# Layer norm of the first token tile: statistics partly on ScalarE, one set of factors, another order of the halves

## The chip, the core and the metric

The kernel runs on one core of a Trainium2 chip. The metric is the device time of one execution in microseconds. A core has five engines that run side by side, each through its own queue in order: PE (TensorE, matrix products and transposes; PEld is its loading of weights), DVE (VectorE), ACT (ScalarE), POOL (GpSimd) and SP, which here only issues transfers. They wait for one another by semaphores. SBUF is the memory that all engines work in, PSUM holds what PE writes, in banks of 128 x 512 values.

## What is computed

2 x 1024 tokens of 512 features, all in float32. Each token is normalised over its features (layer norm). Two paths use the result: a linear layer with a block-masked weight, and a gated feed-forward network with an RMS norm ahead of it. Their product is added to the input.

```python
def _layernorm(x, axis=-1, eps=1e-05):
    m = jnp.mean(x, axis=axis, keepdims=True)
    v = jnp.var(x, axis=axis, keepdims=True)
    return (x - m) / jnp.sqrt(v + eps)

# attn: out = einsum('bsk,nk->bsn', data, weight * block_mask)
# ffn:  nx = x * rsqrt(mean(x*x) + 1e-5) * ln_w
#       g, u = nx @ gate_w.T, nx @ up_w.T          (1792 wide)
#       out = (silu(g) * u) @ down_w.T
xn = _layernorm(L0_attn_data)
s = attn(xn)
g = silu(ffn(xn))
return L0_attn_data + s * g
```

## The kernel before

The 2048 tokens are four token tiles t of 512, each four row tiles i of 128 tokens. A row tile lies in SBUF with tokens on the partitions and 512 features along them. The products need features on the partitions, so a normalised row tile is transposed by PE in four chunks c of 128 features; a chunk of a whole token tile fills one PSUM bank (`pt`, 128 x 512) and is copied to SBUF (`evacuate`).

The products follow Strassen's scheme in Winograd's form, at two levels: instead of eight block products it takes seven and sums of blocks. One outer product q of one group g of weights is an *instance* j; an instance is seven inner products m of 128 x 128 by 128 x 512, which accumulate in banks x, y and z (`instance`, line 395 the product). Instance 0 works on chunks 0 and 1, instance 1 on chunks 2 and 3. In this text x0 is the first product of instance 0, in bank x, with chunk 0 of token tile 0; z0 is its product with chunk 1; x1 and z1 are those of instance 1 with chunks 2 and 3. The later products (y0 and so on) need token tile 1 as well, and differences of chunks that DVE and POOL make (`inner_b`). Bank y of instance 1 (y1) is the one that z1 leaves. The gate weights of both instances are scaled by the RMS weight ahead of use (`scale_a`, line 314 on POOL), and sums of their quarters are made on POOL (`inner_a`, line 98).

Only token tiles 0 and 1 take the way of this text, in the head of the kernel; tiles 2 and 3 follow later under running products. For a tile of the head the steps are:

- `load_x` (line 127): four transfers of 256 KB by SP's queue.
- `stats(t, i)` (lines 131, 132): DVE's bn_stats and bn_aggr give mean and variance of a row tile, into `agg`.
- `factors(t, i, n)` (lines 150, 147, 148): ACT takes the root of the variances of n row tiles, DVE the reciprocal `scl` and the shift `nb`. Token tile 0 has two sets, of row tiles 0, 1 and 2, 3; token tile 1 has one.
- `normalise(t, i, eng, cols)` (line 158 on ACT, line 156 on DVE): half a row tile, 256 features, in place.
- `transpose(t, c, i, tag)` (line 165) and `evacuate(t, c, eng)` (line 173).

Nothing is scheduled by a tool: `at(pos, fn)` notes an event with a position, and at the end the events are issued in order of position. Every engine's queue is the order of its instructions in that list. `T(us)` turns a time into a position, and the list `EARLY` moves single products and copies of the first two instances ((j, m) a product, (j, 0) the seed copy of x). So a position sets the order on an engine, not a time.

Before the head's first real work PE runs products of a unit matrix (`warm`, line 756). On POOL a 1-element memset (line 742) holds back SP's later loads.

Of the kernel before, what the change touches and what calls it, by code (L numbers as in the profile page):

```python
# [8 lines left out]
F32 = mybir.dt.float32  # L9
I32 = mybir.dt.int32  # L10
AF = mybir.ActivationFunctionType
ALU = mybir.AluOpType
AX = mybir.AxisListType

P = 128
W = 512
# [15 lines left out]
def tile_masked_linear_gated_ffn(  # L32
# [11 lines left out]
    nc = tc.nc  # L44
# [15 lines left out]
    small = ctx.enter_context(tc.tile_pool(name="small", bufs=2))  # L60
# [6 lines left out]
    EARLY = {}  # L67

    def at(pos, fn, *args):
        events.append((pos, len(events), fn, args))  # L70
# [5 lines left out]
    mem = big.tile([P, sum(n for _, n in RINGS), W], F32, tag="mem", name="mem")  # L76
# [5 lines left out]
    F = first_slot  # L82
# [6 lines left out]
    def slots(i, n):  # L89
        return mem[:, i : i + n, :]  # L90
# [3 lines left out]
    def bank(tag, name):  # L94
        return ps.tile([P, W], F32, tag=tag, name=name, bufs=PSB[tag])

    def add(eng, o, a, b, op=ALU.add):
        eng.tensor_tensor(o, a, b, op)  # L98

    dve, pool, act = nc.vector, nc.gpsimd, nc.scalar  # L100
# [18 lines left out]
    xt, raw, stat = {}, {}, {}  # L119
    agg = small.tile([P, NTT, TT, 2], F32, tag="agg", name="agg", bufs=1)  # L120
# [8 lines left out]
    def stats(t, i):  # L129
        st = small.tile([P, 6], F32, tag="st", name=f"st_{t}_{i}")  # L130
        nc.vector.bn_stats(st, xt[t, i])  # L131
        nc.vector.bn_aggr(agg[:, t, i, :], st)

    def factors(t, i=0, n=TT):


        if t < 2:
            scl = small.tile([P, n], F32, tag="scl", name=f"scl_{t}_{i}", bufs=3)
            nb = small.tile([P, n], F32, tag="nb", name=f"nb_{t}_{i}", bufs=3)
        else:  # L140
            scl, nb = fac[:, t - 2, 0, :], fac[:, t - 2, 1, :]
        for k in range(n):
            stat[t, i + k] = (scl[:, k : k + 1], nb[:, k : k + 1])
        rows = slice(i, i + n)

        def last():
            nc.vector.reciprocal(scl, scl)
            nc.vector.scalar_tensor_tensor(nb, agg[:, t, rows, 0], -1.0, scl, ALU.mult, ALU.mult)

        return [lambda: nc.scalar.activation(scl, agg[:, t, rows, 1], AF.Sqrt, bias=eps2, scale=1.0 + EPS), last]  # L150

    def normalise(t, i, eng, cols=slice(0, W)):
        scl, nb = stat[t, i]
        v = xt[t, i][:, cols]
        if eng is dve:
            nc.vector.tensor_scalar(v, v, scl, nb, ALU.mult, ALU.add)
            return
        nc.scalar.activation(v, v, AF.Identity, bias=nb, scale=scl)  # L158

# [137 lines left out]
    def w_slots(g):  # L297

        return (F["s"], F["s"] + 5) if g % 2 else (F["q"], F["a1"] + 4)
# [28 lines left out]
    def outer_a(g):  # L328


        b = wblk[g]
        v = {}

        def in_bank(k, K):
            v[k] = bank("V", f"a{k}_{g}")
            scaled(v[k], b[k], g, K)

        return [lambda: scaled(b[2], b[1], g, 0), lambda: scaled(b[4], b[4], g, 1), lambda: in_bank(1, 0),
                lambda: in_bank(0, 0), lambda: add(dve, b[1], v[1], b[4]),
                lambda: add(dve, b[2], v[0], b[2], ALU.subtract), lambda: add(dve, b[0], b[1], v[0], ALU.subtract),  # L340
                lambda: in_bank(3, 1), lambda: add(dve, b[3], v[3], b[0], ALU.subtract)]
# [17 lines left out]
    def mask_a(v, R, K):  # L359
        v = v.rearrange("p (b j) -> p b j", j=BLK)  # L360
        k = keep[:, 2 * R + K, :].unsqueeze(2).to_broadcast([P, 16, BLK])
        nc.gpsimd.tensor_tensor(v, v, k, ALU.mult)

    def inner_a(g, part, k0=0, n=2):

        if part == 1:
            i, si, qs = F["a1"] + 2 * (g % 3), F["s"] + 2 * (g % 2), (1, 2)
        else:
            i, si, qs = *w_slots(g), BLOCKS
        a, s = slots(i + k0, n), slots(si + k0, n)  # L370
        a11, a21, a12, a22 = (a[:, :, k * P : (k + 1) * P] for k in range(4))
        s1, s2, s3, s4 = (s[:, :, k * P : (k + 1) * P] for k in range(4))
        for k in range(n):
            aop[g, qs[k0 + k]] = {1: a11[:, k], 2: a12[:, k], 3: s4[:, k], 4: a22[:, k],
                                  5: s1[:, k], 6: s2[:, k], 7: s3[:, k]}
        return [lambda: add(pool, s1, a21, a22), lambda: add(pool, s2, s1, a11, ALU.subtract),
                lambda: add(pool, s4, a12, s2, ALU.subtract), lambda: add(pool, s3, a11, a21, ALU.subtract)]
# [258 lines left out]
    def down_instance(o, q, where_, prior, dest, after):  # L636
# [78 lines left out]
        if last_set:  # L715
            at(where_(17) + 0.1, base_of_last)
            for part, pos in zip(parts, (where_(23), where_(24), where_(25))):
# [9 lines left out]
    N = len(order)  # L727
    END = 7 * N
    T = lambda us: (us - 14.0) / 0.86
    EARLY.update({(0, 1): T(10.4), (0, 2): T(11.3), (1, 1): T(12.1), (1, 2): T(13.0), (0, 0): T(11.5), (1, 0): 4.3,  # L730
                  (0, "z"): 2.2, (1, "z"): 4.5})
    SILU = 26.2
    at(T(-10), constants)
# [5 lines left out]
    at(T(-10), load_x, 1)  # L739
    at(T(-10), load_a, 0, 1)  # L740

    at(T(9.95), lambda: nc.gpsimd.memset(mem[:, F["a1"] + 2, 0:1], 0.0))
    for K in range(2):
        at(T(9.96), load_a, 1, K)
    at(T(9.96), load_x, 2)
    for K in range(2):
        at(T(9.96), load_a, 2, K)
    at(T(9.96), load_x, 3)
    def plan(pos, step, todo):
        for i, fn in enumerate(todo):  # L750
            at(pos + step * i, fn)


    def warm(n, b):
        for _ in range(n):
            nc.tensor.matmul(b[:, :P], ident, ident, start=True, stop=True, skip_group_check=True)

    at(T(1.4), lambda: warm(22, bank("V", "idle")))
    plan(T(4.9), 0, factors(0, 0, 2))
    plan(T(7.1), 0, factors(0, 2, 2))  # L760
    for t, p, step in ((1, T(12.5), 0), (3, 23.2, 0.6), (2, 36.1, 1.2)):
        plan(p, step, factors(t))
    for us, i, h in ((5.9, 0, 0), (6.0, 0, 1), (6.1, 1, 0), (7.2, 1, 1), (7.95, 2, 0), (8.4, 2, 1), (7.95, 3, 0), (8.4, 3, 1)):
        at(T(us), normalise, 0, i, dve if i == 3 else act, slice(h * W // 2, (h + 1) * W // 2))
    for i in range(TT):
        half = act if i < 2 else dve
        at(T(3.7 + 0.82 * i), stats, 0, i)
        at(T(9.35 + 0.82 * i), stats, 1, i)
        for h, cols in enumerate((slice(0, W // 2), slice(W // 2, W))):
            at(T(13.45 + 0.9 * h + 0.4 * (i % 2)), normalise, 1, i, half, cols)  # L770
        for c in range(KC):
            at(T((8.9, 9.3, 9.8, 11.0)[c] + 0.05 * i), transpose, 0, c, (0, 1, 3, 2)[i], "XYYX"[c])
            at((T(14.35), T(14.8), T(15.25), 4.1)[c] + 0.06 * i, transpose, 1, c, (2, 3, 0, 1)[i], "XVVV"[c])
    at(T(6.0), scale_a, 0, 0, pool)
    at(T(10.0), scale_a, 0, 1, pool)
    for c in range(KC):
        at(T((9.75, 10.3, 10.85, 12.05)[c]), evacuate, 0, c, act)
        at((5.6, 2.09, 6.0, 5.05)[c], evacuate, 1, c, act)
    for pos, q, m, eng in ((1.1, 1, 5, dve), (1.87, 1, 6, dve), (2.56, 1, 7, dve), (3.95, 2, 5, dve), (2.7, 1, 4, pool),
                           (5.06, 2, 6, dve), (10.05, 2, 7, dve), (5.07, 2, 4, pool)):  # L780
# [16 lines left out]
    for n, p0 in ((1, 31), (0, 50)):  # L797
        t = 2 + n
# [24 lines left out]
    for g in range(G + 1):  # L823
        p, rest = 7 * where[g, 1], 7 * where[g, BLOCKS[0]]
        for K in range(2):
            if g > 2:
                at(p - 22, load_a, g, K)
            if g == G:
                at(p - (10.4, 7.3)[K], lambda K=K: mask_a(aq[G, 0, K], 0, K))
            elif g > 1:  # L830
                at(p - (10.4, 7.3)[K], scale_a, g, K)
        if g:
            plan(p - 7, 1, inner_a(g, 1))
        else:
            plan(T(9.9), 0, inner_a(0, 1, 0, 1))
            plan(2.75, 0, inner_a(0, 1, 1, 1))
        at(rest - 29, load_block, g)

        def block_sums(g=g):
            for k, fn in enumerate(outer_a(g)):  # L840
                todo[g, k] = fn
        at(rest - 20, block_sums)
        if g == G:
            for k, (R, K) in ((1, (1, 0)), (4, (1, 1)), (0, (0, 0)), (3, (0, 1))):
                at(rest - 20.5, lambda k=k, R=R, K=K: mask_a(wblk[G][k], R, K))
        for k, off in enumerate((-19.9, -19.3, -18.1, -17, -15.95, -15.94, -15.93, -15.3, -13.95)):
            at(rest + off, lambda g=g, k=k: todo[g, k]())
        plan(rest - 13, 2.5, inner_a(g, 2, 0, 5))
# [138 lines left out]
```

## Time and profile before

| what | us |
|---|---|
| time, median of 3 runs (lowest, highest) | 506.41 (506.39, 506.83) |
| span of the profiled execution, first to last instruction | 504.8 |
| PE busy in 0 to 8.2 us | 6.83 |
| PE busy in 497.4 to 504.8 us | 3.49 |
| row tiles of token tile 0: last landing event of each | 3.48, 4.16, 4.95, 5.58 |
| first weights (instance 0), second (instance 1): landed | 7.29, 11.07 |
| mean of a bn_stats, a bn_aggr (DVE) | 0.67, 0.18 |
| mean of a half row tile normalised on ACT, on DVE | 0.59, 0.42 |
| mean of a chunk's copy on ACT | 0.59 |
| mean of half a weight tile scaled on POOL | 0.96 |
| mean of one 128 x 128 sum on POOL | 0.46 |

The profiled execution is one of its own; the times come from other executions, and their median lies 1.6 us over its span. Lines of a profile are read as: line of the kernel, engine, operation, tile written <- tiles read, shape. PE pieces x2 are the two passes of one float32 product. What an engine waited for is given in brackets with the idle time before it. Instructions of ACT and DVE overlap their neighbours a little, so that a start may lie ahead of the end before it.

### The profile page before, as it was taken

What the parts mean: (1) busy time and instruction counts of PE and PEld (TensorE: products, weight loads), DVE (VectorE), ACT (ScalarE), POOL (GpSimd) and SP (SyncE); (2) the same over time, 40 slices, a digit from 0 to 9 for tenths busy, and PEclk for the clock granted to TensorE, in tenths of its full rate; (3) what the DMA queues carried; (4) which work ended last, traced back from release to release, by engine and by line L of the source; (5) the groups of instructions that cost most, each with busy time, mean ns of one, the idle gap of its engine ahead of it and who ended that gap; (6) DMA issues with size and microseconds to landing.
All of it is one profiled execution on the core that took longest, in us unless ns stands there. A gap on an engine that the chain in (4) does not pass through costs nothing.

```text
span 504.8 us, 4923 instructions
## 1 busy us (share of the span) xinstructions
PE 499.2 (99%) x1231; PEld 227.4 (45%) x1231; DVE 375.6 (74%) x578; ACT 188.1 (37%) x362; POOL 358.8 (71%) x301
## 2 busy tenths in 40 slices
PE   8999999999999999999999999999999999999996
PEld 7444444444444444444444444444444444444444
DVE  6887887876968969697896969879657644377636
ACT  6667775734535363443535333330101101001111
POOL 5629997464886959879696999985672764649960
PEclk9999999999999999999999999999999999999999
DMA  6878746368178594876949475599996798467362
GB/s 208 306 234 335 292 168 250 123 251 293 62 245 295 186 329 181 295 240 244 335 154 317 179 265 213 216 351 387 365 335 221 253 389 311 130 238 269 106 229 84
DMA packets 62221, 124.75 MB, mean 247 GB/s; under 512 B 5968, under 2 KB 13552, under 8 KB 60144
## 3 DMA queue, kind: packets, MB, share of 16 engines
q1 hardware_dynamic: 62048, 124.43, 69.1%
q8 instruction: 10, 0.16, 0.1%
q14 instruction: 19, 0.16, 0.1%
q10 hardware_dynamic: 144, 0.00, 0.0%
HBM read 78.25 MB, written 46.15 MB: 246 GB/s over the span
## 4 chain that ended last, share of the span: by engine, by line
PE 97%; DVE 1%; ACT 1%; DMA 1%; issue 0%; DVEq 0%; ACTq 0%
PE x L395 38%; PE y L395 19%; PE dx L643 15%; PE z L395 10%; PE dy L643 8%; PE dz L643 5%; PE dv L643 1%; PE pt L165 1%; DMA mem<-in_x 1%; DVE mem L98 0%; ACT mem L158 0%; DVE st L131 0%; DVE mem L633 0%; ACT silu L626 0%; ACT scl L150 0%
## 5 line engine op out<-in xcount | busy, mean ns | idle before, releaser
L98 POOL TENSOR_TENSOR mem<-mem 128x512 f32<-128x512 f32 (+4 forms) x261 | 322.1, 1257 | 111.6 <-ACT mem L423 30.5
L395 PE MATMUL x<-mem 128*128 128x512 f32 x448 | 211.7, 593 | 0.0
L395 PEld LDWEIGHTS x<-mem 128*128 128x128 f32 x448 | 84.6, 190 | 107.3 <-issue 89.7
L98 DVE TENSOR_TENSOR mem<-x,mem 128x512 f32<-128x512 f32 x137 | 93.4, 686 | 42.1 <-PE x L395 40.4
L395 PE MATMUL y<-mem 128*128 128x512 f32 x224 | 114.6, 593 | 0.1
L643 PE MATMUL dx<-mem 128*128 128x512 f32 x174 | 78.3, 592 | 0.0
L98 DVE TENSOR_TENSOR mem<-mem 128x1536 f32<-128x1536 f32 (+3 forms) x50 | 66.9, 1342 | 6.9 <-PE dx L643 4.4
L98 DVE TENSOR_TENSOR mem<-y,mem 128x512 f32<-128x512 f32 x96 | 65.9, 686 | 7.9 <-PE y L395 6.5
L402 ACT COPY z<-x 128x512 f32<-128x512 f32 x54 | 30.9, 573 | 94.7 <-PE x L395 91.7
L395 PEld LDWEIGHTS y<-mem 128*128 128x128 f32 x224 | 42.2, 190 | 53.1 <-issue 46.5
L395 PE MATMUL z<-mem 128*128 128x512 f32 x112 | 57.3, 593 | 0.0
L643 PEld LDWEIGHTS dx<-mem 128*128 128x128 f32 x174 | 33.1, 190 | 41.6 <-issue 40.9
L643 PE MATMUL dy<-mem 128*128 128x512 f32 x98 | 44.5, 592 | 0.0
L461 ACT ACTIVATE gate<-mem 128x512 f32<-128x512 f32 x56 | 32.7, 602 | 20.4 <-DVE mem L98 15.9
L466 DVE TENSOR_TENSOR mem<-gate,mem 128x512 f32<-128x512 f32 x56 | 38.1, 682 | 1.9 <-ACT gate L461 1.5
L616 POOL TENSOR_TENSOR mem<-mem 128x512 f32<-128x512 f32 x16 | 25.8, 1619 | 13.6 <-DMA mem<-s_dram 13.4
L626 ACT ACTIVATE silu<-mem 128x512 f32<-128x512 f32 x15 | 9.0, 602 | 64.6 <-DVE mem L98 48.3
L395 PEld LDWEIGHTS z<-mem 128*128 128x128 f32 x112 | 21.1, 190 | 25.9 <-issue 21.4
L98 DVE TENSOR_TENSOR mem<-z,mem 128x512 f32<-128x512 f32 x41 | 28.1, 685 | 2.8 <-PE z L395 2.7
L643 PEld LDWEIGHTS dy<-mem 128*128 128x128 f32 x98 | 18.6, 190 | 23.4 <-issue 23.2
L98 DVE TENSOR_TENSOR mem<-dx,mem 128x512 f32<-128x512 f32 x16 | 11.1, 691 | 20.3 <-PE dx L643 20.2
L643 PE MATMUL dz<-mem 128*128 128x512 f32 x56 | 25.2, 592 | 0.0
(86 smaller groups left out, 286.9 us busy)
## 6 DMA issues: line engine op xcount, KB each, us to landing
h_dram<-mem SPq DMA_DIRECT2D x98, 256.0 KB, 2.2
mem<-h_dram SPq DMA_DIRECT2D x28, 768.0 KB, 6.7
mem<-in_gu SPq DMA_DIRECT2D x42, 256.0 KB, 3.9
acc_dram<-mem SPq DMA_DIRECT2D x8, 1024.0 KB, 4.0
mem<-acc_dram SPq DMA_DIRECT2D x8, 1024.0 KB, 6.1
mem<-in_x_t SPq DMA_DIRECT2D x24, 256.0 KB, 5.5
mem<-in_x SPq DMA_DIRECT2D x16, 256.0 KB, 4.5
s_dram<-mem SPq DMA_DIRECT2D x16, 256.0 KB, 6.1
```

Source lines behind the costliest of these rows:

```text
L98: eng.tensor_tensor(o, a, b, op)
L165: nc.tensor.transpose(pt[t, c][:, i * P : (i + 1) * P], xt[t, i][:, c * P : (c + 1) * P], ident)
L395: nc.tensor.matmul(st[key], weights(g, q, m), operand(q, m), start=first and not (key == "z" and seeded), stop=True, skip_group_check=True)
L402: nc.scalar.copy(st["z"], st["x"])
L461: nc.scalar.activation(gate[key], t(), AF.Silu)
L466: nc.vector.tensor_mul(a(), gate[key], b())
L616: at_later.append(lambda: nc.gpsimd.tensor_tensor(s_tile, s_tile, rms_bc[t], ALU.mult))
L626: nc.scalar.activation(b[0][:, part], y[:, part] if source is None else source(), AF.Silu)
L643: nc.tensor.matmul(st[key], w(), b(), start=first and key != "z", stop=True, skip_group_check=True)
```

## The change

The statistics of row tile 1 of token tile 0 are made by ACT (`stats_act`): a pass with Identity whose accumulator gives minus the scaled mean, a pass with Square, shifted by it, whose accumulator gives the variance, and a one-column multiply for the mean. The passes write scratch values into a slot that is free then. DVE makes the other three. Token tile 0 has one set of factors for its four row tiles. The halves are normalised in another order, and one of them (row tile 1, second half) by POOL. The transposes have positions of their own: of chunks 2 and 3, row tile 0 comes ahead of x0, row tiles 1, 2 and 3 come behind z0. The seed copy of x0 moves behind the normalising of token tile 1. On POOL two of the four weight sums of instance 0 move behind the scaling of the second weights, and the memset and the loads that it holds back have new positions. `warm` has 21 products instead of 22. DVE's statistics of token tile 1 come earlier in the list.

```diff
+    shift = small.tile([P, 1], F32, tag="shift", name="shift", bufs=1)
+
+    def stats_act(t, i):
+
+        v, junk, s = xt[t, i], mem[:, F["q"], :], W ** -0.5
+        nc.scalar.activation(junk, v, AF.Identity, scale=-s / W, accum_out=shift)
+        nc.scalar.activation(junk, v, AF.Square, bias=shift, scale=s, accum_out=agg[:, t, i, 1:2])
+        nc.scalar.mul(agg[:, t, i, 0:1], shift, -1.0 / s)
+
...
-        if eng is dve:
-            nc.vector.tensor_scalar(v, v, scl, nb, ALU.mult, ALU.add)
+        if eng is not act:
+            eng.tensor_scalar(v, v, scl, nb, ALU.mult, ALU.add)
             return
...
-    EARLY.update({(0, 1): T(10.4), (0, 2): T(11.3), (1, 1): T(12.1), (1, 2): T(13.0), (0, 0): T(11.5), (1, 0): 4.3,
+    EARLY.update({(0, 1): T(9.6), (0, 2): T(10.4), (1, 1): T(12.1), (1, 2): T(13.0), (0, 0): T(15.3), (1, 0): 4.3,
...
-    at(T(9.95), lambda: nc.gpsimd.memset(mem[:, F["a1"] + 2, 0:1], 0.0))
+    at(T(10.2), lambda: nc.gpsimd.memset(mem[:, F["a1"] + 2, 0:1], 0.0))
     for K in range(2):
-        at(T(9.96), load_a, 1, K)
-    at(T(9.96), load_x, 2)
+        at(T(10.21), load_a, 1, K)
+    at(T(10.21), load_x, 2)
...
-    at(T(1.4), lambda: warm(22, bank("V", "idle")))
-    plan(T(4.9), 0, factors(0, 0, 2))
-    plan(T(7.1), 0, factors(0, 2, 2))
-    for t, p, step in ((1, T(12.5), 0), (3, 23.2, 0.6), (2, 36.1, 1.2)):
+    at(T(1.4), lambda: warm(21, bank("V", "idle")))
+    plan(T(6.7), 0, factors(0))
+    at(T(4.2), stats_act, 0, 1)
+    for t, p, step in ((1, T(11.9), 0), (3, 23.2, 0.6), (2, 36.1, 1.2)):
         plan(p, step, factors(t))
-    for us, i, h in ((5.9, 0, 0), (6.0, 0, 1), (6.1, 1, 0), (7.2, 1, 1), (7.95, 2, 0), (8.4, 2, 1), (7.95, 3, 0), (8.4, 3, 1)):
-        at(T(us), normalise, 0, i, dve if i == 3 else act, slice(h * W // 2, (h + 1) * W // 2))
+    for us, i, h, eng in ((7.45, 3, 0, dve), (7.46, 2, 0, dve), (7.45, 0, 0, act), (7.95, 1, 0, act), (8.45, 0, 1, act), (9.2, 1, 1, pool),
+                          (9.9, 2, 1, act), (10.4, 3, 1, act)):
+        at(T(us), normalise, 0, i, eng, slice(h * W // 2, (h + 1) * W // 2))
+    for us, i, cs in ((7.96, 3, (0,)), (7.97, 0, (0,)), (7.98, 2, (0,)), (7.99, 1, (0,)), (8.70, 3, (1,)), (8.71, 0, (1,)), (8.72, 2, (1,)),
+                      (8.73, 1, (1,)), (9.05, 0, (2, 3)), (10.5, 1, (2, 3)), (10.51, 2, (2, 3)), (10.52, 3, (2,)), (10.53, 3, (3,))):
+        for c in cs:
+            at(T(us) + 0.0001 * c, transpose, 0, c, i, "XYYX"[c])
     for i in range(TT):
         half = act if i < 2 else dve
-        at(T(3.7 + 0.82 * i), stats, 0, i)
-        at(T(9.35 + 0.82 * i), stats, 1, i)
+        if i != 1:
+            at(T(3.7 + 0.82 * i), stats, 0, i)
+        at(T(8.2 + 0.82 * i), stats, 1, i)
...
-            at(T((8.9, 9.3, 9.8, 11.0)[c] + 0.05 * i), transpose, 0, c, (0, 1, 3, 2)[i], "XYYX"[c])
...
-    at(T(10.0), scale_a, 0, 1, pool)
+    at(T(10.3), scale_a, 0, 1, pool)
     for c in range(KC):
-        at(T((9.75, 10.3, 10.85, 12.05)[c]), evacuate, 0, c, act)
+        at(T((8.95, 9.45, 11.2, 12.1)[c]), evacuate, 0, c, act)
...
-            plan(T(9.9), 0, inner_a(0, 1, 0, 1))
+            for us, fn in zip((9.9, 9.9, 13.0, 13.0), inner_a(0, 1, 0, 1)):
+                at(T(us), fn)
```

More of the change, by code (lines that the diff above doesn't have):

```diff
@@ L740, in tile_masked_linear_gated_ffn @@
     at(T(-10), load_a, 0, 1)
-    at(T(9.95), lambda: nc.gpsimd.memset(mem[:, F["a1"] + 2, 0:1], 0.0))
+    at(T(10.2), lambda: nc.gpsimd.memset(mem[:, F["a1"] + 2, 0:1], 0.0))
     for K in range(2):
-        at(T(9.96), load_a, 1, K)
-    at(T(9.96), load_x, 2)
+        at(T(10.21), load_a, 1, K)
+    at(T(10.21), load_x, 2)
     for K in range(2):
-        at(T(9.96), load_a, 2, K)
-    at(T(9.96), load_x, 3)
+        at(T(10.21), load_a, 2, K)
+    at(T(10.21), load_x, 3)
     def plan(pos, step, todo):
```

## The prediction

> **What bounds the kernel now.** I read the page first: engines and span. PE is busy in 99% of the span, the other engines 37 to 74%.
>
> ```profile
> span 504.8 us, 4923 instructions
> PE 499.2 (99%) x1231; PEld 227.4 (45%) x1231; DVE 375.6 (74%) x578; ACT 188.1 (37%) x362; POOL 358.8 (71%) x301
> ```
>
> Then the busy time by stretch (columns: stretch, its length, busy us and instruction count of each engine, granted PE clock, DMA share, GB/s), to see where PE's few missing microseconds lie.
>
> ```profile
> 8.20:12.50 4.30, 4.04 (x23) 2.34 (x21) 3.95 (x11) 3.90 (x9) 4.06 (x9) 1.00 0.42 151
> 12.50:20.00 7.50, 7.41 (x29) 3.83 (x30) 6.51 (x14) 5.60 (x13) 3.81 (x6) 1.00 0.97 337
> 20.00:497.40 477.40, 477.40 (x1116) 211.26 (x1117) 357.65 (x534) 173.19 (x331) 348.66 (x274) 1.00 0.70 249
> ```
>
> From 20.0 to 497.4 us PE has no gap. The changed code lies ahead of it, so the change moves the end only by moving PE's arrival there. Third, the chain of waits over the head (start, us, what).
>
> ```profile
> 8.31 0.42 DVE mem L156
> 8.78 1.39 PE pt L165 x10
> 10.16 0.95 PE x L395 x2
> 11.11 0.44 PE pt L165 x4
> 11.54 0.86 PE z L395 x2
> 12.41 0.04 issue
> 12.45 1.12 PE x L395 x2
> 13.57 0.90 PE z L395 x2
> 14.47 1.31 PE pt L165 x12
> ...
> 19.83 0.09 issue
> 19.92 1.10 PE y L395 x2
> ```
>
> PE runs in the order of its queue: 12 transposes, x of instance 0 (x0), 4 transposes, z0, x1, z1, 12 transposes, and so on. Its real work there is hardly compressible: a product is two passes of 0.43 us (0.86), a transpose 0.109 us (12 in 1.31). Last, the timeline, for who holds x1 and what stands before it on ACT.
>
> ```profile
> 9.32 1.56 ACT L173 COPY mem<-pt 128x512 f32<-128x512 f32 x3
> 9.51 1.94 POOL L98 TENSOR_TENSOR mem<-mem 128x128 f32<-128x128 f32 x4
> ...
> 11.46 1.83 POOL L314 TENSOR_SCALAR mem<-mem,lnw_sb 128x256 f32<-128x256 f32 x2
> ...
> 12.44 0.30 PEld L395 LDWEIGHTS x<-mem 128*128 128x128 f32 x2 [0.87 <-POOL mem L314]
> ...
> 19.08 0.69 DVE L98 TENSOR_TENSOR mem<-z,mem 128x512 f32<-128x512 f32 x1
> ```
>
> x1 starts when POOL has scaled the first half of its weights (11.46 + 0.93, and 0.05 of release): a gate that better normalising of tokens doesn't open. After z1 a chain of seven DVE operations follows, from the first transposed chunk of token tile 1 to the total of z1, which frees the bank of y1; so all after z1 keeps its distance to z1.
>
> [...] L314, one operation and one pointer, takes 927. [...] one L314 took 1039 instead of 927 beside DVE's L156.
>
> **The change part by part.** Times from the span's start; landings are the last of the 16 landing events of a transfer.
>
> Statistics and factors. One bn_stats and bn_aggr pair leaves DVE (0.82 us), one sqrt, reciprocal and nb set goes. Row tile 0 is counted from 3.50 as before; row tile 2 landed at 4.95, so DVE counts it from 4.97 and row tile 3 from 5.79 (a bn_stats starts 0.10 after the aggregate before it), whose aggregate ends at 6.67. On ACT the tile 1 statistics start at about 4.20 (landed 4.16): [...] The trace has no ACT pass with an accumulator; [...] The sqrt starts at 6.76 (two waits cost 0.09, as at 5.93 to 6.02 before), nb is ready 0.69 later as now (7.58 to 8.27), plus 0.01 for four columns: 7.46.
>
> Normalising. ACT does (0,h0) at 7.55, (1,h0) 8.05, (0,h1) 8.55, one each 0.49 to 0.50, then copies chunk 0 at 9.05 and chunk 1 at 9.53. Chunk 0 was copied at 9.32: 0.27 gained, and 2 and 3 (h0) on DVE are done by 8.3. x0 follows the end of that copy (9.64) by 0.10: 9.74 against 10.01. One warming product fewer is not felt: it ends at about 7.95, when the first transpose becomes possible.
>
> PE's order. z0 now directly follows x0: 9.74 + 0.94 = 10.68 to 11.54. The last six transposes of chunks 2 and 3 (row tiles 1, 2, 3), which before lay ahead of x0 or between x0 and z0, stand behind z0: 11.54 to 12.19. The same work stands ahead of x1 as before, but with the copy of chunk 2 at its end. Before, that copy was done at 10.89; x1 reads it. Now the fifth of the six transposes starts at 11.98 and ends at 12.25 (0.273 each); ACT copies 12.29 to 12.88; x1 starts at 12.95 at the earliest. Against 12.45 that is 0.50 later, 0.76 of PE idle behind the transposes, where 0.2 were.
>
> What is queued behind that wait on ACT: the sqrt of token tile 1 (its statistics are ready at 11.5 by DVE, 0.8 earlier than now, but nothing uses that), at 12.77; the copy of chunk 3, 12.97 to 13.56; the normalising of tile 1 from 13.5 instead of 13.10; then the seed copy of x0 (moved from 11.15). z1 needs chunk 3 at 13.91: in time. The transposes of tile 1 start at 14.81 instead of 14.31, and their halves are ready (ACT h0 by 14.1 and 14.6, h1 by 15.6). The seed ends near 16.2, before DVE's total of z0 (16.36 + 0.5). So nothing further adds, and nothing absorbs: +0.50 at x1 is +0.50 at 19.92.
>
> POOL. The half (1,h1) stands where two of the four weight sums stood: L314 ends at 9.43, the half runs 9.51 to 10.44, two sums to 11.51, then L314 for x1's weights at 11.52 instead of 11.46: first half done at 12.45, second at 13.38. x1 could go at 12.50, z1 at 13.43, both before chunk 2 lets them. The other two sums run 13.4 to 14.3, when POOL was idle until 16.59. This needs the half to cost one L314 (0.93). [...] I take 0.93; up to 1.4 is hidden behind chunk 2.
>
> SP and DMAs. The loads behind POOL's memset move from 11.39 to 11.5; the order of SP's queue is the same. The mask's load now also waits for ACT's scratch writes, done at 5.6, 12 us earlier than its issue at 17.98. Nothing.
>
> Sum: -0.27 at x0, overtaken by +0.50 at x1. 504.8 + 0.5 = 505.3 for the span; the median of runs lies 1.6 over the profiled span (506.41), hence 506.9.
>
> **The rivals.**
> 1. Nothing remains: ACT has chunk 2 as early as POOL's weights, so x1 goes at 12.5: 506.4. For it: the gate of POOL stands in both kernels, and x0 comes earlier. Against: PE can't take the transposes ahead of z0, and its pace is known.
> 2. Slower: POOL's half with two pointers and two operations costs more than 1.4 us; from there each 0.1 is 0.1 on x1. At 1.9: sums end at 12.48, x1's weights at 13.42 and 14.35, z1 at 14.43 instead of 13.41: +1.0, 507.4; at 2.4, 507.9. For it: L314 at 256 elements is dearer (927) than a two-tensor sum of 256 (728), so its scalar path isn't cheap. [...]
> 3. Slower: ACT's passes last. If Identity, Square and their read-outs together pass 2.3 us, the one sqrt for all four row tiles waits for them; at 1.4 each, +0.5 more: 507.4. For it: the accumulator isn't in the trace. [...]
> 4. A gain of over 1 us, 505.2: x1 would have to start by 11.4, before its weights are scaled. Only something outside this reading gives it.
>
> **How the numbers follow.** Forecast 506.9 with 0.58 (its own range 506.5 to 507.3), rival 1 0.15, rival 2 0.13, rival 3 0.08, rival 4 0.06. What a measurement of this kernel can tell from no change is about 0.2%, 1.0 us: 505.4 to 507.4. Rival 4 is faster: 0.06. Slower: two thirds of rivals 2 and 3 (0.14) and the upper edge of the forecast, where the small costs taken as nothing add (0.10): 0.24. Within: 0.70. The range takes rival 1 and the bounds of POOL and ACT: 506.0 to 507.9.
>
> **What would show it.** Right: x0 near 9.75, z0 at once behind it, six transposes, an idle PE of some 0.7 us put down to ACT's copy, x1 near 12.95, and the gapless stretch 0.5 later. POOL's L165 row gives its price at once; ACT's L139 and L140 rows, and whether the sqrt's wait ends by DVE or ACT, decide rival 3. Wrong: x1 released by POOL, or PE's clock under 1.00 in the stretches to 20 us.

## The result, and the profile after

| | before | after |
|---|---|---|
| median of 16 runs each (lowest, highest), us | 506.81 (506.39, 507.40) | 507.68 (507.27, 508.38) |
| ratio after / before, 95% interval | | 1.0019 (1.0012 to 1.0025) |
| span of the profiled execution, us | 504.8 | 505.5 |

The changed kernel is slower by about 0.9 us (0.6 to 1.3). The forecast was a loss of 0.5, and 506.9 as the time. The kernel before has 506.81 here, where the three runs that the forecast started from gave 506.41. The page of the changed kernel begins:

```profile
span 505.5 us, 4924 instructions
...
PE 499.4 (99%) x1229; PEld 227.7 (45%) x1229; DVE 376.1 (74%) x574; ACT 188.9 (37%) x365; POOL 359.1 (71%) x302
```

PE's work is the same, and the span grew. The busy time by stretch of the changed kernel shows in which stretch (columns as before: stretch, length, busy us and instructions of PE, PEld, DVE, ACT, POOL, then PE's clock, DMA share, GB/s):

```profile
8.20:12.50 4.30, 4.24 (x26) 2.86 (x24) 3.21 (x9) 2.94 (x6) 3.83 (x8) 1.00 0.64 214
12.50:20.00 7.50, 6.89 (x29) 3.80 (x28) 5.83 (x13) 6.46 (x14) 3.33 (x7) 1.00 1.01 362
20.00:497.40 477.40, 477.32 (x1116) 210.70 (x1115) 359.60 (x535) 173.89 (x333) 349.03 (x276) 1.00 0.69 248
```

In the first row PE is less idle than before (4.24 busy of 4.30, was 4.04). The second row gives more than that back: 6.89 of 7.50, was 7.41, so 0.52 us more of idle PE. From 20 us on nothing differs but where the stretch lies. The chain of waits of the changed kernel (start, us, what) names the place:

```profile
12.41 0.43 POOL mem L98
12.84 0.35 issue
13.19 1.10 PE x L404 x2
14.28 0.86 PE z L404 x2
...
20.59 1.10 PE y L404 x2
```

x1 starts at 13.19 (12.45 before, +0.74) and y1 at 20.59 (19.92 before, +0.67), which is what the span grew by. (Lines of the changed kernel stand nine higher from `factors` on: L159 is the root, L165 to L167 normalise, L174 transposes, L182 copies, L323 scales weights, L404 multiplies.) By the chain x1 waited for POOL's sum of L98. The timeline of the changed kernel (start, us, engine, line, operation; in brackets the idle time before it and its inferred releaser) says otherwise:

```profile
8.64 1.25 PE L174 MATMUL pt<-ident,mem 128*128 128x128 f32 x10
8.64 0.55 POOL L165 TENSOR_SCALAR mem<-mem,scl,nb 128x256 f32<-128x256 f32 x1
...
9.28 1.07 ACT L182 COPY mem<-pt 128x512 f32<-128x512 f32 x2 [0.20 <-PE pt L174]
...
9.96 1.10 PE L404 MATMUL x<-mem 128*128 128x512 f32 x2
...
10.59 1.82 POOL L323 TENSOR_SCALAR mem<-mem,lnw_sb 128x256 f32<-128x256 f32 x2 [0.40 <-DMA mem<-in_gu]
...
10.90 1.02 PE L404 MATMUL z<-mem 128*128 128x512 f32 x2
...
11.76 0.82 PE L174 MATMUL pt<-ident,mem 128*128 128x128 f32 x6
...
12.38 0.86 POOL L98 TENSOR_TENSOR mem<-mem 128x128 f32<-128x128 f32 x2
12.50 0.58 ACT L182 COPY mem<-pt 128x512 f32<-128x512 f32 x1 [1.17 <-PE pt L174]
...
13.16 0.30 PEld L404 LDWEIGHTS x<-mem 128*128 128x128 f32 x2 [0.82 <-POOL mem L98]
13.19 0.58 ACT L182 COPY mem<-pt 128x512 f32<-128x512 f32 x1
13.19 1.10 PE L404 MATMUL x<-mem 128*128 128x512 f32 x2 [0.61 <-POOL mem L98]
```

x1 needs the first of POOL's two scalings (the L323 pair, 10.59 to 12.41, so the first ended near 11.5) and chunk 2. The sums of L98 are for later products. The copy of chunk 2 runs 12.50 to 13.09, and the loading of x1's weights into PE (PEld) begins 0.07 later. That copy waits for the six transposes, and they for z0. Whether POOL or the copy is the releaser had to be settled by runs.

### The profile page after: what moved, and what is told of

It reads as the page before. It is cut to its first block, busy times and chain, and to the rows that moved or that the text cites. A ratio compares the mean times of both kernels' runs of the same rounds, so it can differ in the third digit from the quotient of the medians.

```text
span 505.5 us, 4924 instructions
## 1 busy us (share of the span) xinstructions
PE 499.4 (99%) x1229; PEld 227.7 (45%) x1229; DVE 376.1 (74%) x574; ACT 188.9 (37%) x365; POOL 359.1 (71%) x302
## 4 chain that ended last, share of the span: by engine, by line
PE 96%; DMA 1%; DVE 1%; POOL 0%; SPq 0%; issue 0%; ACT 0%; DVEq 0%; POOLq 0%
PE x L404 38%; PE y L404 19%; PE dx L652 15%; PE z L404 9%; PE dy L652 8%; PE dz L652 5%; PE dv L652 1%; DMA mem<-in_gu 1%; DMA mem<-in_x 1%; DVE mem L98 0%; POOL mem L323 0%; PE pt L174 0%; SPq L127 0%; DVE mem L642 0%; ACT silu L635 0%
## 5 line engine op out<-in xcount | busy, mean ns | idle before, releaser
L98 POOL TENSOR_TENSOR mem<-mem 128x512 f32<-128x512 f32 (+4 forms) x261 | 322.2, 1259 | 112.4 <-ACT mem L432 30.4
L404 PE MATMUL x<-mem 128*128 128x512 f32 x448 | 211.7, 593 | 0.7 <-POOL mem L98 0.6
L404 PEld LDWEIGHTS x<-mem 128*128 128x128 f32 x448 | 84.4, 190 | 107.7 <-issue 90.4
L98 DVE TENSOR_TENSOR mem<-x,mem 128x512 f32<-128x512 f32 x137 | 93.4, 686 | 41.7 <-PE x L404 40.0
L404 PE MATMUL y<-mem 128*128 128x512 f32 x224 | 114.6, 593 | 0.1
L98 DVE TENSOR_TENSOR mem<-mem 128x1536 f32<-128x1536 f32 (+3 forms) x50 | 68.5, 1375 | 7.7 <-PE dy L652 2.6
L98 DVE TENSOR_TENSOR mem<-y,mem 128x512 f32<-128x512 f32 x96 | 65.9, 686 | 8.0 <-PE y L404 6.6
L404 PEld LDWEIGHTS y<-mem 128*128 128x128 f32 x224 | 42.2, 190 | 53.1 <-issue 46.3
L404 PE MATMUL z<-mem 128*128 128x512 f32 x112 | 57.2, 593 | 0.0
L404 PEld LDWEIGHTS z<-mem 128*128 128x128 f32 x112 | 21.2, 190 | 26.3 <-issue 22.1
L98 DVE TENSOR_TENSOR mem<-z,mem 128x512 f32<-128x512 f32 x41 | 28.1, 685 | 2.8 <-PE z L404 2.7
L98 DVE TENSOR_TENSOR mem<-dx,mem 128x512 f32<-128x512 f32 x16 | 11.0, 690 | 19.9 <-PE dx L652 19.9
```

The source lines that it names most:

```text
L404: nc.tensor.matmul(st[key], weights(g, q, m), operand(q, m), start=first and not (key == "z" and seeded), stop=True, skip_group_check=True)
```

## The experiments

The expectations call the reading above (chunk 2, copied behind z0 and six transposes, holds x1) theory A, and the chain's reading (POOL holds x1) theory B; other rivals are described where they come up. Each ratio is to the kernel before, run beside it, with its 95% interval. Starts in us, from the profile of each run; landings of transfers, further down, are their last landing events in the trace:

| run | ratio | x0 | x1 | x1 - x0 | y1 |
|---|---|---|---|---|---|
| before | 1 | 10.01 | 12.45 | 2.44 | 19.92 |
| after | 1.0019 (1.0012 to 1.0025) | 9.96 | 13.19 | 3.23 | 20.59 |
| z0_last | 1.0006 (0.9998 to 1.0014) | 10.24 | 12.81 | 2.57 | 20.14 |
| before_order | 1.0013 (1.0006 to 1.0020) | 10.06 | 13.28 | 3.22 | 20.68 |
| pool_two_ops | 1.0020 (1.0013 to 1.0027) | 9.88 | 13.10 | 3.22 | 20.50 |
| dve_stats | 1.0016 (1.0010 to 1.0023) | 9.96 | 13.18 | 3.22 | 20.59 |
| warm17 | 1.0015 (1.0008 to 1.0021) | 9.79 | 13.01 | 3.22 | 20.42 |
| before_warm17 | 1.0002 (0.9995 to 1.0009) | 10.26 | 13.29 | 3.03 | 20.77 |
| before_pool2 | 0.9996 (0.9987 to 1.0004) | 10.05 | 12.28 | 2.23 | 19.84 |
| before_pool2_t1 | 1.0008 (1.0000 to 1.0016) | 10.17 | 12.40 | 2.23 | 20.11 |
| z0_pool2_warm17 | 1.0004 (0.9996 to 1.0012) | 10.20 | 12.76 | 2.56 | 20.09 |
| dve_halves | 1.0009 (1.0003 to 1.0016) | 11.25 | 13.19 | 1.94 | 21.16 |

A profile is one execution, and the landings in it move all starts. Those of before_warm17 (507.53, median 506.90) and dve_halves (508.28, median 507.40, the longest of its 21 runs) come from executions well above their medians. The column x1 - x0 is free of the landings of the row tiles and therefore steadier; late weights can still move it, as in before_warm17.

### The order undone in the changed kernel

z0 behind the six transposes instead of ahead of them; nothing else differs from the changed kernel:

```diff
-    EARLY.update({(0, 1): T(9.6), (0, 2): T(10.4), ...
+    EARLY.update({(0, 1): T(9.6), (0, 2): T(10.54), ...
```

> The changed kernel with one position moved: z0 stands behind the six transposes of chunks 2 and 3. Theory A (the copy of chunk 2, which waits for transposes behind z0, holds x1): the copy starts near 11.5 us instead of 12.50 and lies under z0; x1 follows z0 or POOL's weights, at 12.2 to 12.6 instead of 13.19; the time falls by 0.5 to 0.9 us against the changed kernel, to 1.0001 to 1.0009 of the kernel before. Theory B (as the chain of waits names it, POOL's sums and weights hold x1): the order on PE doesn't matter, ratio 1.0019 as with the whole change.

The timeline of this run:

```profile
10.24 1.10 PE L404 MATMUL x<-mem 128*128 128x512 f32 x2
...
11.18 0.93 PE L174 MATMUL pt<-ident,mem 128*128 128x128 f32 x6
...
11.60 1.82 POOL L323 TENSOR_SCALAR mem<-mem,lnw_sb 128x256 f32<-128x256 f32 x2 [0.36 <-DMA mem<-in_gu]
...
11.95 1.02 PE L404 MATMUL z<-mem 128*128 128x512 f32 x2
12.04 0.59 ACT L182 COPY mem<-pt 128x512 f32<-128x512 f32 x1 [0.42 <-PE pt L174]
...
12.69 0.31 PEld L404 LDWEIGHTS x<-mem 128*128 128x128 f32 x2 [0.55 <-POOL mem L323]
12.81 1.02 PE L404 MATMUL x<-mem 128*128 128x512 f32 x2
```

The copy of chunk 2 now lies beside z0 (12.04 to 12.62), and x1 follows z0 after its two passes (11.95 + 0.86 = 12.81) with no gap of PE. POOL scaled x1's weights a full microsecond later than in the changed kernel (11.60 against 10.59), and x1 still came 0.38 earlier. This speaks for A and against B. It also rules out the sums of L98, which POOL made behind both scalings, from 13.39 on, when x1 was running. By the middle values it gives back about two thirds of the loss, 1.0019 to 1.0006.

### The order alone, in the kernel before

The reverse. The front of the kernel before stays as it was: two sets of factors, its statistics, its halves, its warming, its order on POOL. Only PE's and ACT's order around x1 becomes that of the change:

```diff
-    EARLY.update({(0, 1): T(10.4), (0, 2): T(11.3), (1, 1): T(12.1), (1, 2): T(13.0), (0, 0): T(11.5), (1, 0): 4.3,
+    EARLY.update({(0, 1): T(10.4), (0, 2): T(11.25), (1, 1): T(12.1), (1, 2): T(13.0), (0, 0): T(15.3), (1, 0): 4.3,
...
-    for t, p, step in ((1, T(12.5), 0), ...
+    for t, p, step in ((1, T(11.9), 0), ...
...
-            at(T((8.9, 9.3, 9.8, 11.0)[c] + 0.05 * i), transpose, 0, c, (0, 1, 3, 2)[i], "XYYX"[c])
+            late = 9.8 if i == 0 else 11.3 + 0.05 * i
+            at(T((8.9 + 0.05 * i, 9.3 + 0.05 * i, late, late + 0.01)[c]), transpose, 0, c, (0, 1, 3, 2)[i], "XYYX"[c])
...
-        at(T((9.75, 10.3, 10.85, 12.05)[c]), evacuate, 0, c, act)
+        at(T((9.75, 10.3, 11.6, 12.05)[c]), evacuate, 0, c, act)
```

> The kernel before with the changed order of PE and ACT around x1 alone, and nothing of the front: its two sets of factors, its statistics, its halves, its POOL order and its warming stay. z0 stands directly behind x0; of chunks 2 and 3 only row tile 0 is transposed ahead of x0, the other six transposes stand behind z0; the copy of chunk 2 follows them, then the root of token tile 1; the seed copy of x0 stands behind the normalising. Theory A (the copy of chunk 2 behind z0 and six transposes holds x1, and this order is the cause of the half microsecond): x0 at about 10.0, z0 at 10.95, the six transposes to 12.5, x1 at about 13.2 where the kernel before has 12.45, all later starts 0.5 to 0.8 later; ratio to the kernel before 1.0010 to 1.0016. Rival (the order costs nothing by itself; the loss comes from the front, which hangs everything on the last row tile, or from the warming): x1 at 12.5, ratio 0.9995 to 1.0004. If it costs as much as the whole change, the front brought nothing; if less, the front cost the rest.

The timeline of this run (lines as in the kernel before):

```profile
10.06 1.10 PE L395 MATMUL x<-mem 128*128 128x512 f32 x2
...
10.99 1.02 PE L395 MATMUL z<-mem 128*128 128x512 f32 x2
...
11.72 1.82 POOL L314 TENSOR_SCALAR mem<-mem,lnw_sb 128x256 f32<-128x256 f32 x2 [0.15 <-DMA mem<-in_gu]
...
11.85 0.82 PE L165 MATMUL pt<-ident,mem 128*128 128x128 f32 x6
...
12.60 0.59 ACT L173 COPY mem<-pt 128x512 f32<-128x512 f32 x1 [2.15 <-PE pt L165]
...
13.28 1.10 PE L395 MATMUL x<-mem 128*128 128x512 f32 x2 [0.61 <-POOL mem L314]
```

x0 is where it was (10.06, against 10.01), and x1 comes at 13.28, 0.83 later than before. Part of the 0.83 is not the order: the second weights landed at 11.63 instead of 11.07 in this execution, and with POOL alone as the gate x1 would have started near 12.69, by an estimate (11.72 + 0.92, and the 0.05 of release that the kernel before had). That leaves 0.59 for the order. The distance x1 - x0 is 3.22, that of the changed kernel (3.23). The view again names POOL as the releaser, but the first of its two scalings (0.92) ended at 12.65; the copy ended at 13.18. With no other part of the change in it, this costs 0.13% (0.06 to 0.20), some 0.66 us. The rival, that the order costs nothing by itself, falls.

Both runs give the same share: the order alone costs 0.13%, and taking it out of the change leaves 0.06%; together the 0.19% of the change. The intervals are 0.07 to 0.08% to each side, so the share of the order is shown, and that of the rest (0 to 0.14%) is not separated from nothing.

### POOL as the releaser

POOL's weight scaling is given a second operation that changes no value:

```diff
-                nc.gpsimd.tensor_scalar(o[:, cols], a[:, cols], w, None, ALU.mult)
+                nc.gpsimd.tensor_scalar(o[:, cols], a[:, cols], w, 0.0, ALU.mult, ALU.add)
```

> The changed kernel with POOL's scaling of the weights as multiply and add of 0.0 instead of multiply alone, the same result. In the changed kernel POOL took 545 ns for a half row tile with two pointers and two operations, 927 for the scaling with one of each, on the same shape. If the single-operation form itself is the slow one, L323 falls to about 0.55 us. Theory A: x1 is held by ACT's copy, so the time stays at 1.0019 of before, within 0.0007. Theory B (POOL holds x1): x1 comes 0.4 to 0.7 us earlier and the ratio falls to about 1.0008.

The groups of POOL between 5 and 14 us in this run (line, operation, shapes, count | busy us, mean ns | idle before, releaser), and under them its timeline:

```profile
L323 POOL TENSOR_SCALAR mem<-mem,lnw_sb 128x256 f32<-128x256 f32 x4 | 1.9, 498 | 4.7 <-DMA mem<-in_gu 4.7
...
L165 POOL TENSOR_SCALAR mem<-mem,scl,nb 128x256 f32<-128x256 f32 x1 | 0.6, 576 | 0.0
```

```profile
12.19 0.87 POOL L98 TENSOR_TENSOR mem<-mem 128x128 f32<-128x128 f32 x2
12.41 0.59 ACT L182 COPY mem<-pt 128x512 f32<-128x512 f32 x1 [1.16 <-PE pt L174]
...
13.10 1.10 PE L404 MATMUL x<-mem 128*128 128x512 f32 x2 [0.61 <-POOL mem L98]
```

A scaling takes 498 ns instead of 944, and POOL has finished both halves of the second weights by 12.2. x1 comes 0.09 earlier, but so does x0 (0.08), and x1 - x0 stays at 3.22: the weights don't hold it. This run alone doesn't clear the sums of L98, which end at 13.06, next to x1's start. The run warm17 (below) does, with the same order around x1 and the same distance of 3.22; there they begin behind it:

```profile
13.01 1.10 PE L404 MATMUL x<-mem 128*128 128x512 f32 x2 [0.61 <-issue]
...
13.19 0.88 POOL L98 TENSOR_TENSOR mem<-mem 128x128 f32<-128x128 f32 x2
```

What stays the same is the copy: in after, before_order, pool_two_ops, dve_stats, warm17, z0_last and z0_pool2_warm17 the loading of x1's weights into PE begins 0.07 us after the end of the copy of chunk 2. Theory B falls; the time is that of the changed kernel.

### The statistics on ScalarE

Row tile 1's statistics go back to DVE, all else of the change stays:

```diff
-    at(T(4.2), stats_act, 0, 1)
...
+        else:
+            at(T(4.1), stats, 0, 1)
```

> The changed kernel with the statistics of row tile 1 back on DVE, all else as changed. By the trace DVE waited for row tile 2 to land (4.9 us) and would fill most of that gap with row tile 1: the last aggregate ends at 6.8 instead of 6.6, the sqrt and all behind it 0.1 to 0.2 later. Theory A: the loss is not in the statistics; ratio 1.0017 to 1.0026. Rival: the statistics on ACT cost something (its scratch writes or its read-outs): the ratio falls towards 1.0010. If they had brought 0.8 us, as a whole pair taken off DVE would: 1.0035.

1.0016 against 1.0019, intervals that overlap almost wholly, and in the profile x0 at 9.96 and x1 at 13.18 as with ACT. A ratio of 1.0035 lies far outside; a small cost of ACT's passes can't be told from nothing. Of the 0.82 us of statistics that ACT takes over, 0.26 shows at the root (6.71 with ACT, 6.97 without; 0.09 of it is a later landing of row tile 0 in the run without), because with ACT DVE waits 0.44 for row tile 2 to land. In these two executions nothing of it reached x0: with ACT the first transposes stood behind the warming (8.64), without it they started at 8.32 and ACT's halves came later, and the copy of chunk 0 began at 9.28 and 9.27. What ACT's two passes cost is seen in the timeline of the changed kernel:

```profile
4.19 0.63 ACT L139 ACTIVATE mem<-mem 128x512 f32<-128x512 f32 x1 [1.98 <-DMA mem<-in_x]
...
4.73 0.19 ACT L139 ACTIVATION_READ_ACCUMULATOR mem<-mem 128x1 f32 x1
4.91 0.69 DVE L131 BATCH_NORM_STATS2 st<-mem 128x6 f32<-128x512 f32 x1 [0.44 <-DMA mem<-in_x]
4.95 0.72 ACT L140 ACTIVATE mem<-mem,shift 128x512 f32<-128x512 f32 x1
5.58 0.19 ACT L140 ACTIVATION_READ_ACCUMULATOR mem<-mem,shift 128x1 f32 x1
...
5.67 0.19 ACT L141 ACTIVATE agg<-shift 128x1 f32<-128x1 f32 x1
5.74 0.66 DVE L131 BATCH_NORM_STATS2 st<-mem 128x6 f32<-128x512 f32 x1
...
6.43 0.18 DVE L132 BATCH_NORM_AGGREGATE agg<-st 128x2 f32<-128x6 f32 x1
...
6.71 0.30 ACT L159 ACTIVATE scl<-agg,eps 128x4 f32<-128x4 f32 x1 [0.86 <-DVE agg L132]
```

Each accumulator is read out by an instruction of its own, 187 ns. ACT was still done 0.76 us ahead of DVE (5.85 and 6.61).

### The warming

In the profile of the changed kernel the first transposes stood behind the warming products, so these were made fewer, in the changed kernel and in the kernel before:

```diff
-    at(T(1.4), lambda: warm(21, bank("V", "idle")))
+    at(T(1.4), lambda: warm(17, bank("V", "idle")))
```

> The changed kernel with 17 warming products instead of 21. In the changed kernel's trace the clock was granted at 6.6 us, not at 5.2 as in the trace of before, and the warming ran until 8.6 us, 0.7 after the first half row tile was ready. Theory C (part of the loss is that warming now runs into the first transposes): the first transposes start near 7.9 us, x0 at 9.7 instead of 9.97, the ratio falls by 0.0003 to 0.0007 to some 1.0014. Rival: the warming has slack on average[...]: ratio 1.0019 or more.

```diff
-    at(T(1.4), lambda: warm(22, bank("V", "idle")))
+    at(T(1.4), lambda: warm(17, bank("V", "idle")))
```

> The kernel before with 17 warming products instead of 22. Theory C: before, the transposes waited for DVE's half at 8.7 us, so a late clock cost less than in the changed kernel: ratio 0.9995 to 1.0000. If both kernels lose alike to a late clock, it falls as much as warm17 does against the changed kernel.

In the changed kernel the transposes began at 8.01 instead of 8.64 and x0 came at 9.79 instead of 9.96, but the time was 507.65 against 507.68: 1.0015 and 1.0019 can't be told apart. In the kernel before nothing is shown either (1.0002). Its profile has a late y1 (20.77) for another reason: the first weights landed at 8.22 instead of 7.29, POOL scaled them late, made its four sums until 12.30, and came to the second weights, which had landed at 11.54, only then:

```profile
8.42 1.85 POOL L314 TENSOR_SCALAR mem<-mem,lnw_sb 128x256 f32<-128x256 f32 x2 [4.48 <-DMA mem<-in_gu]
...
10.36 1.94 POOL L98 TENSOR_TENSOR mem<-mem 128x128 f32<-128x128 f32 x4
...
12.31 1.83 POOL L314 TENSOR_SCALAR mem<-mem,lnw_sb 128x256 f32<-128x256 f32 x2
```

So a cost of the warming is seen in one trace and not in the times.

### In search of a version better than both

POOL's faster form (the edit of pool_two_ops, here at line 314), put into the kernel before, where POOL does hold x1:

> The kernel before with POOL's scaling as multiply and add of 0.0, the form that took 0.48 us instead of 0.93. Here POOL does hold x1 (12.45 us in its profile, 13.29 in another one where the weights landed 0.5 us later), by theory A: x1 can go when z0 has been issued, 12.24 at the earliest, so the time falls by 0.2 us and by more where the weights land late: ratio 0.9985 to 0.9996. If what held x1 before was not POOL, nothing changes: 1.0000.

The timeline of this run:

```profile
12.28 1.02 PE L395 MATMUL x<-mem 128*128 128x512 f32 x2
...
13.35 2.08 ACT L158 ACTIVATE mem<-mem,nb,scl 128x256 f32<-128x256 f32 x4 [0.45 <-DVE nb L148]
...
14.00 1.81 PE L165 MATMUL pt<-ident,mem 128*128 128x128 f32 x12
...
15.64 1.09 PE L395 MATMUL y<-mem 128*128 128x512 f32 x2
```

x1 came directly behind z0, 0.17 earlier than in the kernel before, but y0 only 0.05 earlier (15.64, was 15.69): twelve transposes that need 1.31 now take 1.81, since they wait for the four halves that ACT normalises. The expected gain is not seen in the time: 0.9996 (0.9987 to 1.0004) is no difference. The same kernel with one of ACT's two row tiles of token tile 1 given to POOL:

```diff
-        half = act if i < 2 else dve
+        half = (act, pool, dve, dve)[i]
```

> The kernel before with two edits of POOL and ACT alone: POOL scales the weights in the form of two operations (mult, then add of 0), which took 0.5 instead of 0.93 us, so x1 is no longer held by it; and row tile 1 of token tile 1 is normalised by POOL instead of ACT, so that ACT has two halves there instead of four. With the first edit alone x1 came 0.17 earlier in the profile and y0 did not, since the halves of token tile 1 held the transposes. If those halves are the next wait: x1 at 12.3, the twelve transposes done by about 15.3 instead of 15.8, y0 at 15.4 and y1 at 19.6, ratio 0.9990 to 0.9998. If a third wait stands right behind (the chunk that DVE copies and the sums of POOL ahead of y1): y0 earlier but y1 at 19.8 to 19.9, ratio 0.9996 to 1.0004. If DVE's scaling beside POOL slows down: y0 at 15.7 or later, ratio 1.0000 to 1.0006.

The diff leaves out `normalise`, which gets the changed kernel's branch for POOL. POOL's halves took 0.69 and 0.57, but DVE's own four, beside them, went from 410 ns each to 508, as its group from 13 to 16 us in this run shows:

```profile
L156 DVE TENSOR_SCALAR mem<-mem,scl,nb 128x256 f32<-128x256 f32 x4 | 1.8, 508 | 0.0
```

The transposes took 1.72, and y0 came 3.48 behind x1, where it came 3.36 behind it without that edit. y0 waited for DVE's first sum of L98, which followed DVE's halves at 15.15, where it began at 14.86 without that edit. The expectation's third case is the one that the trace shows: what ACT gains DVE loses. The time, 1.0008, is no gain.

Two combinations on the side of the change. The first is z0_last, pool_two_ops and warm17 in one, with the three edits shown above:

> The changed kernel with z0 behind the six transposes, POOL's scaling with two operations and 17 warming products. Theory A: now neither the copy of chunk 2 nor POOL holds x1, it follows z0 without a gap near 12.2 to 12.5; ratio 0.9990 to 1.0003. If single costs just add to other waits: 1.0006, as with z0 moved alone.

x1 follows z0 without a gap (11.90 + 0.86 = 12.76), later than expected, since x0 came at 10.20. The time comes near the kernel before, and not below it (1.0004). The second keeps the faster form and the 17 products and takes the late halves of row tiles 2 and 3 to DVE, with their transposes ahead of x0:

```diff
-                          (9.9, 2, 1, act), (10.4, 3, 1, act)):
+                          (7.48, 2, 1, dve), (7.47, 3, 1, dve)):
...
-                      (8.73, 1, (1,)), (9.05, 0, (2, 3)), (10.5, 1, (2, 3)), (10.51, 2, (2, 3)), (10.52, 3, (2,)), (10.53, 3, (3,))):
+                      (8.73, 1, (1,)), (9.03, 3, (2, 3)), (9.04, 2, (2, 3)), (9.05, 0, (2, 3)), (10.3, 1, (2, 3))):
...
-        at(T((8.95, 9.45, 11.2, 12.1)[c]), evacuate, 0, c, act)
+        at(T((8.95, 9.45, 11.2, 11.85)[c]), evacuate, 0, c, act)
```

> The changed kernel with the second halves of row tiles 2 and 3 on DVE, right behind their first halves; their transposes of chunks 2 and 3 ahead of x0, row tile 1's between x0 and z0; the copy of chunk 3 ahead of the sqrt; POOL's scaling with two operations, 17 warming products. Theory A: x0 at 9.9, the copy of chunk 2 near 11.1 under z0, x1 at 11.9 to 12.1, limited by PE's own order and the landing of the weights; y0 near 15.3; the statistics of token tile 1 come 0.7 later, ready near 12.1, in time. Ratio 0.9980 to 0.9995. If DVE's later statistics become the wait (transposes of token tile 1 after 13.9), the gain is halved.

x1 follows z0 without a gap (12.33 + 0.86 = 13.19), but DVE's four scalings took 598 ns each beside POOL instead of 410 and stand ahead of the transposes that x0 waits for, so x0 moved to 11.25 (row tiles 2 and 3 also landed 0.9 late in that execution, the longest of its runs). The expectation of 0.9980 to 0.9995 was missed: 1.0009 (1.0003 to 1.0016). None of these kernels is faster than the kernel before.

## Why the prediction was right, and where its sum was too small

**The number.** The forecast's own range was 506.5 to 507.3, and 507.68 lies above it. It lies inside the whole range, 506.0 to 507.9, whose upper part was there for rivals 2 and 3; these did not occur, so in that the number was luck. Of the 0.77 between 506.41 + 0.50 and 507.68, 0.40 is the kernel before, taken from three runs (506.41, in sixteen 506.81), and 0.37 is the loss itself, 0.87 instead of 0.50.

**Right: the place and the mechanism.** x0, z0, six transposes, an idle PE, the copy of chunk 2, x1: that is the order seen. The distance from x0 to x1 was worked out as 12.95 - 9.74 = 3.21; the trace has 3.23, and the order alone in the kernel before has 3.22. The idle PE behind the transposes was put at 0.76; counted in the same way, from 11.76 + 6 x 0.109 = 12.41 to 13.19, it is 0.78 (the view, which counts the last transpose to its end, has 0.61).

**Right: rivals 2 and 3 don't occur.** POOL's half was taken at 0.93, and at 1.9 in rival 2; it took 0.55. That ACT's statistics end ahead of DVE's was my estimate; the trace of before has no such pass. They ran from 4.19 to 5.85: the two passes took 629 and 721 ns and their read-outs 187 each, 1.72 together where rival 3 needed more than 2.3, and DVE came last, 0.76 later. The forecast of nb at 7.46 was 7.41.

**Right: the loss is carried on.** x1 +0.74, y1 +0.67. Between the two 0.07 was absorbed where the sum had nothing.

**Wrong in size: the term "-0.27 at x0".** The sum was -0.27 for the front and +0.77 for the order (3.21 against 2.44), +0.50. The runs show about +0.66 for the order, from both sides, so that term was right within its error. The front's gain isn't there: x0 came at 9.96 instead of 9.74 in the profile, a gain of 0.05. In the times z0_last, which keeps the front, measures +0.06% (-0.02 to +0.14); with -0.27 at x0, and 0.13 for its somewhat longer way to x1 (2.57, was 2.44), it should have had -0.14 us or -0.03%, just outside. The step that failed in the trace is "One warming product fewer is not felt: it ends at about 7.95". Its last pass began at 8.53 and the first transpose at 8.64, hence the copy of chunk 0 at 9.28 instead of 9.05, which is the whole 0.22 of x0. The times don't show this cost (warm17), so it explains the trace and not the median. One product fewer should have ended sooner, but the trace's record of the granted clock begins at 6.61 us, where the kernel before had 5.15, and until then a warming pass followed the one before it by 0.213 us instead of 0.112. I had counted the products and taken their pace from one execution. The start of that record differs from execution to execution: over the twelve profiles it lay between 4.42 and 7.03 us, and between 4.42 and 6.61 in the four with 21 products.

**Open: a second part of that term.** The landings were taken from the same one execution. With one set of factors x0 hangs on row tile 2, the third to land: DVE stands idle until it is there (0.44 us in the lines above) and counts row tile 3, which has then landed, straight after it. Where the warming isn't in the way, x0 follows the landing of row tile 2 by 4.81 to 4.82 us (z0_last 5.43 and 10.24; pool_two_ops 5.06 and 9.88; warm17 4.98 and 9.79; z0_pool2_warm17 5.38 and 10.20). With two sets it hung on the first row tile, by 6.53 to 6.64 (before 3.48 and 10.01; before_pool2 3.51 and 10.05; before_order 3.53 and 10.06; before_warm17 3.62 and 10.26); only in before_pool2_t1, where row tile 1 landed late (4.43) and DVE waited for it, it was 6.92. The mean landings of the twelve profiles are 5.18 and 3.52, against 4.95 and 3.48 in the execution that I worked from. By these means x0 would be at 10.0 with one set and 10.1 with two, so 0.1 of gain is left of 0.27. With it the sum is -0.1 + 0.77, about +0.67, inside the measured 0.6 to 1.3. This is read from the traces across runs; no run held the landings still, so it is argued and not shown. The warming run moved the trace by 0.17 at x0 and the median by 0.03, so it doesn't decide between the two parts.

## What to carry to other kernels

On an engine that runs in order, as PE does here, moving a product ahead also moves a later copy behind it (in before_order the copy of chunk 2 started at 12.60, behind z0, where it had been done by 10.89, and the order cost 0.13%): put the producers of the copy that is needed next ahead of the product that can hide that copy, even if the product could start sooner. Where a change makes everything hang on a later one of several arrivals, work with the spread of the arrivals over several executions (0.96 us for the third row tile here), not with the ones of a single profile. Where an instruction waits for several things, the releaser that a view names is an inference: move that one by itself, and see whether the wait moves.

## What the hardware showed that I had not expected

- On POOL, a 128 x 256 float32 TENSOR_SCALAR with one operation and one pointer took 927 to 1039 ns in the kernel before and 944 in the mean in the changed kernel; with two operations it took 477 to 685 ns, whether the second operand was a constant (477 in the mean in before_pool2_t1, 498 in pool_two_ops) or a pointer (545 in the changed kernel, 685 and 573 beside DVE in before_pool2_t1). The form with less work was the slower one. The prediction had taken the half with two pointers and two operations at 0.93, the time of the form with one of each.
- DVE's TENSOR_SCALAR of the same shape went from 410 ns to 508 (before_pool2_t1) and 598 (dve_halves) in the mean of four beside POOL's work.
- Each of the two accumulators on ACT cost a separate instruction of 187 ns; the passes themselves took 629 ns (128 x 512, immediates only) and 721 ns (one pointer).
- The start of the full granted TensorE clock in the trace's record moved by 2.6 us between executions (4.42 to 7.03), the landing of the third row tile by 0.96 (4.88 to 5.84) and of the fourth by 0.93 (5.58 to 6.51), with the same loads ahead of them.
